# Holding a planner's order on four engines, norms on another engine, and a hidden state laid out by batch, in a four-layer graph network

## The chip, the cores and the metric

The kernel runs on one core of a Trainium2 chip. A core has five engines with a queue each: TensorE (PE; its weight loads are listed as PEld), VectorE (DVE), ScalarE (ACT), GpSimd (POOL) and SyncE (SP), which here issues transfers. The metric is the time of one execution on the device in microseconds (us); the median of three runs before the change is 2407.23 us (2405.26 to 2409.41).

## The reference, cut to what matters

x is 128 batches of 64 nodes with 256 features, adj a 64 by 64 matrix. Four layers follow each other, each as x = layernorm(x + layer(x)):

```python
# layer 0: graph convolution with two batch norms over all 128*64 rows
agg = A_hat @ x;  h = relu(bn(agg @ W1.T + b1));  out = bn(h @ W2.T + b2)
# layer 1: spectral convolution, 4-head attention masked by adj, MLP
h  = relu(ln((L_norm @ x) @ Wc + bc) * g1 + be1);  x1 = h + x
x2 = ln(x1 + attention(x1) @ Wo + bo) * g2 + be2
y  = ln(x2 + gelu(x2 @ W1 + b1) @ W2 + b2) * g3 + be3
# layer 2: two graph convolutions, then four LSTMs one after the other on windows of nodes
h = relu(adj @ (relu(adj @ (x @ Wg0 + bg0)) @ Wg1 + bg1))
for p in 1, 2, 3, 4:       # a window is p neighbouring nodes; its last node gets the LSTM's last state
    h[:, p-1::p] = lstm_p(windows of p nodes of h)
# layer 3: graph attention (one head), residual and norm
```

L_norm needs the largest eigenvalue of a 64 by 64 Laplacian, for which a power of the matrix is formed at the start. All is fp32.

## The kernel before

**Tiles.** The 128 batches are cut into 16 blocks of 8; a block's x is 128 rows by 4 by 256 (`X[i]`, "token-major"), and its hidden state is as large (`H[i]`). Eight spare tiles of the same size (`t`) and, as they come free, tiles of x, h and old weights make up a stock `mem`; PSUM is a stock of four tiles `ps`. The names in the profile are those of the tiles: x, h, t, ps, wA, wB, wL and so on.

**A planner in Python.** The kernel is written as generators ("tasks"): `first_block` and `second_block` (layer 0, a batch norm ends each), `end_block` (layer 0's last norm), `block` (layer 1), `gcn_block` (layer 2's convolutions and LSTM 1 of a block), `unit` (LSTMs 2 to 4 on a group of 32 batches), `last_block` (layer 3). Each `yield step(engine, us, ...)` announces the next piece of work on T (PE), V (VectorE), S (ScalarE), G (POOL) or Q (a transfer) with a cost in us. The loop `flow` keeps up to six blocks in flight, simulates the engines' times by these costs, and always lets that task go on whose next piece can start first; the instructions of the piece are then emitted. It is called twice: for layer 0, and for all the rest. A table change on ScalarE is charged 1.3 us.

**Who sets the order on the chip.** What `flow` emits is a program, not yet the queues. The compiler's scheduler takes the instructions of all engines and orders each engine's queue by its own model of their times; the emitted order is only its priority. In the trace an engine works its queue off in that order, so an instruction that waits for its input holds what stands behind it.

**Norms.** `stats` (L272 to L274) does the statistics on VectorE; then POOL raises the variance to the power -0.5 (L282, L294, L308). Three helpers apply the norm: `ln_steps` (VectorE, L285), `ln_affine_steps` (VectorE, two operations per 256 columns, L297 and L300, with gamma and beta in them), and `ln_steps_act` (a small `ln_nm` on VectorE, L311, then ScalarE, L314). `block` uses `ln_affine_steps` twice, for g1/be1 and g3/be3.

**The hidden state.** From the end of `gcn_block` on, h of a group of 32 batches is one tile seen as `hT`, "p (c n b)": for each of two halves of the features, node by node, with the 32 batches side by side. LSTM 1 writes into it across (L1357, its step is 32 elements). `unit` reads the s-th node of each window (`x_of`) as runs of 32 batches and writes the last node (L1389). PE reads these inputs in the first step's products (L1055), in the product "A11" of the seven products that stand for eight (L1127, a variant of Strassen's method), and in `plain_steps` (L1264). The differences T1 (POOL, L1147) and T3 (VectorE, L1173) read them too. `last_block` copies a block of hT back into batch order with two ScalarE copies (L1467) before it transposes it.

**Lines that the prediction names.** L741: batch norm 2 on ScalarE in `end_block`. L776: relu and residual. L784: copy of the transposed x1. L822, L915, L916, L933: whole-tile operations on POOL. L898: residual after attention. L928: gelu. L1171, L1228: VectorE operations with both inputs in SBUF.

Of the kernel before, what the change touches and what calls it, by code (L numbers as in the profile page):

```python
# [15 lines left out]
P = 128  # L16
# [3 lines left out]
NT = 4  # L20
# [13 lines left out]
def kernel(ctx: ExitStack, tc: tile.TileContext, a: dict, out: bass.AP):  # L34
    nc = tc.nc
    V, S, G, T = nc.vector, nc.scalar, nc.gpsimd, nc.tensor

# [92 lines left out]
    def flow(streams, margin):  # L130
# [92 lines left out]
    hT = [t.rearrange("p (c n b) -> p c n b", c=2, n=N) for t in Hg]  # L223
# [53 lines left out]
    def ln_steps(y):  # L277

        yield step("V", 2.45)
# [3 lines left out]
        yield step("V", 1.9)  # L283
# [5 lines left out]
    def ln_affine_steps(y, g, b):  # L289

        yield step("V", 2.45)
        mv, rs = stats(y)
        yield step("G", 1.0)
        G.tensor_tensor(rs, rs, neghalf[:, :NT], ALU.pow)  # L294
        yield step("V", 3.4)
        for t in range(NT):
            V.scalar_tensor_tensor(y[:, t, :], y[:, t, :], mv[:, t, 0:1], g, ALU.subtract, ALU.mult)  # L297
            o = b if len(b.shape) == 2 else b[:, t, :]
            dst = y if len(b.shape) == 2 else b
            V.scalar_tensor_tensor(dst[:, t, :], y[:, t, :], rs[:, t : t + 1], o, ALU.mult, ALU.add)  # L300

    def ln_steps_act(y):

        n = y.shape[1]
        yield step("V", 0.6 * n)
        mv, rs = stats(y)
        yield step("G", 1.0)
        G.tensor_tensor(rs, rs, neghalf[:, :n], ALU.pow)  # L308
        yield step("V", 0.2)
        nm = sm.tile([P, n], F32, tag="ln_nm", name="ln_nm")  # L310
        V.scalar_tensor_tensor(nm, mv[:, :, 0], -1.0, rs, ALU.mult, ALU.mult)  # L311
        yield step("S", 0.6 * n)
        for t in range(n):
            S.activation(  # L314
                y[:, t, :], y[:, t, :], AF.Identity, scale=rs[:, t : t + 1], bias=nm[:, t : t + 1]
            )
# [89 lines left out]
    with c0:  # L406
# [129 lines left out]
        def bn_coeffs(name, nch, st, g, be):  # L536
# [4 lines left out]
            yield step("V", 0.3 * nch)  # L541
# [16 lines left out]
        def first_block(i):  # L558
# [6 lines left out]
            yield step("T", 1.15, ps=1, sl=1)  # L565
# [25 lines left out]
        def second_block(i):  # L591
# [27 lines left out]
            yield step("S", 2.8)  # L619
# [6 lines left out]
            yield step("V", 1.4, sl=2)  # L626
# [6 lines left out]
            yield step("G", 1.3, waits=False)  # L633
            G.tensor_tensor(T4, h[:, :, u], T2, ALU.subtract)
            yield step("V", 0.7)
# [98 lines left out]
    def end_block(i):  # L734
# [4 lines left out]
        yield step("S", 1.4)  # L739
# [15 lines left out]
    def block(i):  # L755
        x = X[i]
        mark("begun", i)
        yield step("T", 1.15, ps=1, sl=1)
# [15 lines left out]
        yield from ln_affine_steps(y, rows[:, names.index("g1"), :], rows[:, names.index("be1"), :])  # L774
        yield step("V", 1.25)
# [25 lines left out]
        yield step("T", 3.6, ps=1, sl=1)  # L801
# [19 lines left out]
        yield step("G", 2.4, waits=False)  # L821
# [3 lines left out]
        yield step("T", 1.15, ps=1, sl=1)  # L825
# [17 lines left out]
        yield step("V", 1.4, ps=-1)  # L843
# [5 lines left out]
        yield step("V", 2.5)  # L849
# [9 lines left out]
        yield step("G", 1.9)  # L859
# [13 lines left out]
        yield step("T", 1.15, ps=1, sl=1)  # L873
# [40 lines left out]
        yield step("G", 4.7, waits=False)  # L914
# [3 lines left out]
        for hf in range(2):  # L918
# [6 lines left out]
            yield step("S", 1.4, ps=-1, waits=hf == 1, tbl="gelu")  # L925
# [6 lines left out]
        yield step("G", 2.4, waits=False)  # L932
# [17 lines left out]
        yield from ln_affine_steps(y, rows[:, names.index("g3"), :], x)  # L950
# [25 lines left out]
    V.tensor_tensor(bl, bl, bh, ALU.add)  # L976

    def gcn_rows():
# [15 lines left out]
        PS.give(ps)  # L994
        mark("rows")
# [25 lines left out]
    def hT_block(i):  # L1021

        return hT[i // 4][:, :, :, (i % 4) * 8 : (i % 4) * 8 + 8]

    def lstm(p, n, parts, x_of, out_of):
# [4 lines left out]
        v_us, g_us, s_us = (0.05 + n * r for r in (1.25e-3, 2.3e-3, 1.15e-3))  # L1030
# [50 lines left out]
        for c in range(2):  # L1081
            if c:
                tb, sb = yield from gates(((0, 1), (2, 1)), *other)
            t, sl = (tb, sb) if c else (ta, sa)
            t = yield step("G", g_us, at=t, waits=False)
            G.tensor_tensor(of(s_cell)[:, c], of(sl)[:, 0], of(sl)[:, 1], ALU.mult)
            tc_.append(t)
        t_o, s_o = yield from gates(((3, 0), (3, 1)), *to)
        s_h = None
        for c in range(2):  # L1090
# [5 lines left out]
            t = yield step("V", v_us, at=max(t, t_o), sl=0 if p == 1 or c else 1, waits=False)  # L1096
# [39 lines left out]
        for s in range(1, p):  # L1136
# [3 lines left out]
            t_1 = yield step("G", g_us, sl=2, at=0.0, waits=False)  # L1140
# [28 lines left out]
            def differences():  # L1169
                yield step("V", two_us, at=h_at, waits=False)  # L1170
                V.tensor_tensor(T2, h_v, T1, ALU.subtract)  # L1171
                t_h.append((yield step("V", two_us, at=h_at, waits=False)))
                V.tensor_tensor(shaped(T3), shaped(h_v), x_v, ALU.subtract)  # L1173
                t_h.append((yield step("G", g_us, at=t_h[1], waits=False)))
# [44 lines left out]
            t_g = yield step("G", 2 * g_us, at=at[2], waits=False)  # L1219
# [7 lines left out]
            yield step("V", 2 * v_us, at=at[1], waits=False)  # L1227
            V.tensor_tensor(cell, cell, of(act[1]), ALU.mult)  # L1228
            mem.give(act[1])
            t = yield step("V", 2 * v_us, at=t_g, waits=False)  # L1230
# [6 lines left out]
            t = yield step("V", 2 * v_us, at=max(t, at[3]), sl=0 if last else 1, waits=False)  # L1237
# [12 lines left out]
    def plain_steps(p, n, us, of, bias, x_of, shaped, last_h, s_cell, s_h, h_at):  # L1250

        v_us, g_us, s_us = (0.05 + n * r for r in (1.25e-3, 2.3e-3, 1.15e-3))
        for s in range(1, p):
# [20 lines left out]
            for c in range(2):  # L1274
# [4 lines left out]
                tg = yield step("G", g_us, at=ta, waits=False)  # L1279
                G.tensor_tensor(A[:, 1], A[:, 0], A[:, 1], ALU.mult)  # L1280
                t = yield step("V", v_us, at=tb, waits=False)
                V.tensor_tensor(cell, cell, F[:, 0], ALU.mult)
                t = yield step("V", v_us, at=max(t, tg), waits=False)
# [5 lines left out]
            for c, t, sa, sb in ends:  # L1289
                t = yield step("V", v_us, at=t, sl=0 if last or c else 1, waits=False)  # L1290
# [15 lines left out]
    def gcn_block(i):  # L1306
        yield step("T", 1.15, ps=1, sl=1)
# [21 lines left out]
        yield step("T", 1.15, ps=1, sl=1)  # L1329
# [12 lines left out]
        yield step("V", 1.4, ps=-1)  # L1342
# [13 lines left out]
        def out_of(q, c, o, th):  # L1356
            V.tensor_tensor(  # L1357
                hT_block(i)[:, c, :, :].rearrange("p n b -> p b n"), o, th, ALU.mult
            )
# [8 lines left out]
    def unit(p, g, w0, nw, b0, nb):  # L1368
        src = hT[g][:, :, w0 * p : (w0 + nw) * p, b0 : b0 + nb].rearrange("p c (w q) b -> p c w q b", q=p)

        hn = nw * nb // 2
        even = nw % 2 == 0
        parts = [(slice(q * hn, (q + 1) * hn), nw // 2 if even else nw) for q in range(2)]
        if nb < BG:
            parts = [(slice(0, 2 * hn), nw)]

        def half(ap, q):
# [3 lines left out]
            if even:  # L1381
                return ap[..., q * nw // 2 : (q + 1) * nw // 2, :]
            return ap[..., q * nb // 2 : (q + 1) * nb // 2]

        def x_of(s, q):
            return half(src[:, :, :, s, :], q)

        def out_of(q, c, o, th):
            V.tensor_tensor(half(src[:, c, :, p - 1, :], q), o, th, ALU.mult)  # L1389
# [22 lines left out]
    def sum_weights(p, sums):  # L1412
# [18 lines left out]
        for k in range(2):  # L1431
            i0, i1, h0, h1 = (w[:, k, :, c, :] for w in (ih, hh) for c in range(2))
            s1, s2, s3, s4 = (gates(sums[2 * i + k]) for i in range(4))
            for dst, y, z, op in (
# [5 lines left out]
                yield step("V", 0.7)  # L1440
# [15 lines left out]
    def last_block(i, t0=0, nt=NT):  # L1456
# [6 lines left out]
        yield step("S", 2.2 * r, sl=1)  # L1463
        s_h = mem.take()
        hb = fm(mem[s_h])[:, :, : nt * P]
        for c in range(2):
            S.copy(  # L1467
                hb[:, c, :].rearrange("p (b n) -> p b n", n=N),
                hT_block(i)[:, c, :, 2 * t0 : 2 * (t0 + nt)].rearrange("p n b -> p b n"),
            )  # L1470
# [3 lines left out]
        to_tm(px, hb)  # L1474
        mem.give(s_h)
# [13 lines left out]
        yield step("S", 0.3 + 1.1 * r, ps=-1)  # L1489
# [7 lines left out]
        for t in range(0, nt, 2):  # L1497
# [20 lines left out]
            yield step("S", 0.7, ps=-1, waits=False)  # L1518
# [5 lines left out]
        yield step("G", 0.1 + 0.5 * r, sl=1)  # L1524
# [9 lines left out]
        yield step("V", 0.3 + 1.2 * r, ps=-1)  # L1534
# [6 lines left out]
        yield step("S", 0.3 * nt, tbl="exp")  # L1541
# [3 lines left out]
        yield step("V", 0.3 + 0.3 * r)  # L1545
        V.reciprocal(sums[:, :nt], sums[:, :nt])
        V.tensor_tensor(e, e, bc_last(sums[:, :nt], N), ALU.mult)
        yield step("T", 0.1 + 0.5 * r, ps=1)
# [8 lines left out]
        yield step("T", 0.1 + 0.95 * r, ps=1)  # L1557
# [113 lines left out]
    def last_of(i, *part):  # L1671
# [17 lines left out]
        MARGIN,  # L1689
    )  # L1690
# [48 lines left out]
```

## Time and profile before

| what | value |
|---|---|
| median of the runs shown | 2407.23 us (2405.26 to 2409.41) |
| profiled execution: its own time | 2409.44 us |
| profiled execution: span from first to last instruction | 2407.7 us |
| PE busy, of the span | 2287.2 us (95%) |
| VectorE, ScalarE, POOL busy | 1287.7, 1187.4, 591.7 us |
| mean granted clock of PE | 0.982 |
| chain that ended last: PE, VectorE, ScalarE, POOL | 60%, 16%, 7%, 3% |
| ScalarE table loads in the largest group (L928) | 18 of 1283 ns |

Times are read from one profiled execution. A "busy" share is the union of an engine's instructions; a matmul in fp32 stands as two records. The page's slices are fortieths of the span, some 60 us each, with one digit (tenths) per engine; a window gives the same for any stretch. A timeline row is: start, duration, engine, source line, operation, output and inputs, shape, how many are merged, and in brackets how long the engine was idle before and what ended that. "The chain that ended last" is followed back from the last instruction. The clock is what the chip granted PE, as a share of full speed.

### The profile page before, as it was taken

Reading aid. Unit: us, or ns where it says so; the run is one execution under the profiler, and the core shown is the slowest. Engines: PE = TensorE matmul, PEld = TensorE weight load, DVE = VectorE, ACT = ScalarE, POOL = GpSimd, SP = SyncE. Lnnn points to the kernel's source line nnn. Section 1 sums busy time; section 2 is a strip of 40 time slices with the busy share of each in tenths; the row PEclk is TensorE's granted clock in tenths of the full one; section 3 lists DMA queues with packets and bytes.
Section 4 is the critical chain, followed back from the end, with each engine's and each line's share of the span. In section 5 each row is a group of like instructions: output and inputs, shape, how many; then the busy total and the mean of one; then the engine's idle time right before and its main releaser. Section 6 shows DMA issues by size and latency. Waiting matters only on the chain.

```text
span 2407.7 us, 40603 instructions
## 1 busy us (share of the span) xinstructions
PE 2287.2 (95%) x16916; PEld 1759.9 (73%) x16916; DVE 1287.7 (53%) x2904; ACT 1187.4 (49%) x2189; POOL 591.7 (25%) x441
## 2 busy tenths in 40 slices
PE   8999788999989999999999999999999999998997
PEld 4548665666665666666667788899999888887785
DVE  4557678566483474744643433454444444455546
ACT  2257643544434544335453443444444653468766
POOL 0012134232242232331321222222221222122122
PEclk9999899999999999999999999999999999999998
DMA  6100301000000000001000000000001000001111
GB/s 162 49 1 1 111 23 49 28 10 10 1 12 17 10 10 10 1 10 36 36 19 27 18 1 1 17 2 1 1 1 36 1 10 9 19 27 66 40 36 45
DMA packets 42633, 57.91 MB, mean 24 GB/s; under 512 B 6224, under 2 KB 35536, under 8 KB 42448
## 3 DMA queue, kind: packets, MB, share of 16 engines
q1 hardware_dynamic: 41344, 54.22, 7.0%
q8 instruction: 133, 2.18, 0.4%
q10 hardware_dynamic: 1104, 1.08, 0.1%
q14 instruction: 52, 0.43, 0.1%
HBM read 38.52 MB, written 16.78 MB: 23 GB/s over the span
## 4 chain that ended last, share of the span: by engine, by line
PE 60%; DVE 16%; ACT 7%; POOL 3%; issue 2%; POOLq 0%; ACTq 0%; DVEq 0%
PE ps L1127 26%; PE ps L1055 11%; PE ps L365 7%; PE ps L377 4%; PE ps L938 4%; DVE ln_st L272 3%; ACT x L314 2%; PE ps L808 2%; POOL ln_rs L308 1%; PE ps L1507 1%; DVE x L300 1%; PE ps L341 1%; DVE ln_mv L273 1%; PE ps L353 1%; DVE ln_nm L311 1%
## 5 line engine op out<-in xcount | busy, mean ns | idle before, releaser
L1127 PE MATMUL ps<-x,x 128*128 128x256 f32 x928 | 225.0, 380 | 0.7 <-DVE t L1195 0.7
L1127 PEld LDWEIGHTS ps<-x,x 128*128 128x128 f32 x928 | 173.5, 190 | 24.9 <-issue 1.6
L314 ACT ACTIVATE x<-x,ln_nm,ln_rs 128x256 f32<-128x256 f32 x212 | 112.3, 592 | 133.3 <-DVE ln_nm L311 131.9
L1127 PE MATMUL ps<-t,x 128*128 128x256 f32 x672 | 163.7, 380 | 0.0
L1127 PEld LDWEIGHTS ps<-t,x 128*128 128x128 f32 x672 | 126.4, 190 | 17.1 <-DVE x L1195 0.8
L308 POOL TENSOR_TENSOR ln_rs<-ln_rs,neghalf 128x4 f32<-128x4 f32 (+1 forms) x72 | 71.2, 990 | 212.0 <-DVE ln_rs L274 186.4
L365 PE MATMUL ps<-t,W1T 128*128 128x512 f32 x256 | 117.8, 607 | 0.0
L1055 PE MATMUL ps<-h,wL 128*128 128x192 f32 (+2 forms) x480 | 103.9, 371 | 4.8 <-ACT h L1353 4.8
L272 DVE BATCH_NORM_STATS2 ln_st<-x 128x6 f32<-128x256 f32 x260 | 99.7, 403 | 0.4
L1055 PEld LDWEIGHTS ps<-h,wL 128*128 128x128 f32 x480 | 75.6, 192 | 29.9 <-issue 22.5
L294 POOL TENSOR_TENSOR ln_rs<-ln_rs,neghalf 128x4 f32<-128x4 f32 x32 | 36.9, 1153 | 217.1 <-DVE ln_rs L274 217.0
L1055 PE MATMUL ps<-h,x 128*128 128x256 f32 x384 | 86.7, 380 | 2.2 <-ACT t L1067 1.8
L1067 ACT ACTIVATE t<-ps,bih 128x512 f32<-128x512 f32 (+3 forms) x98 | 57.2, 634 | 55.8 <-PE ps L1055 55.1
L1203 ACT ACTIVATE x<-x,bih 128x512 f32<-128x512 f32 (+2 forms) x69 | 44.6, 648 | 80.3 <-DVE x L1193 80.0
L1186 DVE COPY x<-ps 128x256 f32<-128x256 f32 (+2 forms) x69 | 26.1, 378 | 108.4 <-PE ps L1127 107.6
L365 PEld LDWEIGHTS ps<-t,W1T 128*128 128x128 f32 x256 | 47.6, 195 | 49.6 <-issue 49.5
L365 PE MATMUL ps<-t,wA 128*128 128x512 f32 x160 | 76.8, 626 | 5.5 <-ACT t L784 5.5
L1055 PEld LDWEIGHTS ps<-h,x 128*128 128x128 f32 x384 | 72.6, 190 | 12.9 <-ACT t L1067 2.2
L1186 DVE COPY t<-ps 128x256 f32<-128x256 f32 (+2 forms) x51 | 18.8, 373 | 103.8 <-PE ps L1127 103.5
L1067 ACT ACTIVATE x<-ps,bih 128x512 f32<-128x512 f32 (+3 forms) x86 | 51.5, 650 | 40.6 <-PE ps L1055 40.4
L273 DVE BATCH_NORM_AGGREGATE ln_mv<-ln_st 128x2 f32<-128x6 f32 x448 | 71.3, 167 | 0.0
L1193 DVE TENSOR_TENSOR x<-ps,x 128x512 f32<-128x512 f32 (+2 forms) x69 | 41.4, 602 | 53.0 <-PE ps L1127 43.6
(714 smaller groups left out, 5713.2 us busy)
## 6 DMA issues: line engine op xcount, KB each, us to landing
t<-in_x_dram SPq DMA_DIRECT2D x26, 512.0 KB, 4.3
xd<-x SPq DMA_DIRECT2D x16, 512.0 KB, 2.6
x<-xd SPq DMA_DIRECT2D x8, 512.0 KB, 3.3
out_dram<-x SPq DMA_DIRECT2D x8, 512.0 KB, 2.9
h<-in_x_dram SPq DMA_DIRECT2D x5, 512.0 KB, 5.2
wL<-in_L_gnn_Wih_dram SPq DMA_DIRECT2D x2, 1024.0 KB, 5.0
x<-in_L_gnn_Whh_dram SPq DMA_DIRECT2D x2, 1024.0 KB, 5.4
x<-xd SPq DMA_DIRECT2D x5, 256.0 KB, 2.9
```

The costliest lines, as they stand in the source:

```text
L272: V.bn_stats(st[:, t, :], y[:, t, :])
L273: V.bn_aggr(mv[:, t, :], st[:, t, :])
L308: G.tensor_tensor(rs, rs, neghalf[:, :n], ALU.pow)
L314: S.activation(y[:, t, :], y[:, t, :], AF.Identity, scale=rs[:, t : t + 1], bias=nm[:, t : t + 1])
L365: T.matmul(ps[:, c, :], w[:, k, (off + c) * P : (off + c + 1) * P], yT[:, k, :], start=(k == 0), stop=(k == nk - 1),)
L377: T.matmul(ps[:, t, :], yT[:, k, t * P : (t + 1) * P], w[:, k, :], start=(k == 0), stop=(k == nk - 1),)
L808: T.matmul(pv[r * N : (r + 1) * N, b, :, :], x1T[:, k, b * N : (b + 1) * N], Wv_par[:, k, r, :, :], start=(k == 0), stop=(k == 1),)
L938: T.matmul(tm(PS[ps])[:, t, :], fm(mem[gs[k // 2]])[:, k % 2, t * P : (t + 1) * P], W2[:, k, :], start=(k == 0), stop=(k == 3),)
L1055: T.matmul(spread(fm(PS[ps])[:, j, :n], q), WL[p][0][:, k, m], x_of(0, q)[:, k], start=(k == 0), stop=(k == 1),)
L1067: S.activation(of(sl)[:, j], fm(PS[ps])[:, j, :n], AF.Tanh if g == 2 else AF.Sigmoid, bias=bias(g, c))
L1127: T.matmul(dst, WS[p][name](k, g), y[:, k], start=first and k == 0, stop=k == 1, skip_group_check=not first)
L1186: V.tensor_copy(y[:, 1, :], v[:, 0, :])
```

## The change

Five things, of which only the first three change what is executed; the others change the planner's choices.

1. **The order of emission is held** on PE, VectorE, ScalarE and POOL: the compiler's scheduler no longer reorders these queues. SP's queue is still the scheduler's.
2. **Layer 1's norms go to ScalarE**: `ln_affine_steps` is gone; `ln_steps_act` is used, and gamma and beta follow as whole-tile operations on VectorE.
3. **h by batch**: `hT` becomes "p (c b n)": for each batch its 64 nodes side by side. LSTM 1 writes it contiguously; `unit` reads and writes every p-th element; units are halved by batches; `last_block` needs no copy, its two ScalarE copies and their tile are gone.
4. **The planner knows two more things.** Steps of VectorE and POOL that are tagged "m" (two SBUF inputs) don't start on VectorE while a tagged POOL step runs. A change of the matmuls' shape ("quarter", "columns" or whole) is charged 0.1 us. The second `flow` starts its clocks where layer 0 ended instead of at 0.
5. **Costs are adjusted** in some thirty steps, by up to a few tenths of a us each. The sum of two LSTM biases is emitted later, in `gcn_rows`.

The diff, cut to its core:

```diff
+    E = mybir.EngineType
+    ctx.enter_context(tc.manual_schedule(engines={E.PE, E.DVE, E.Activation, E.Pool}))
...
-        free = dict.fromkeys("TVSGQ", 0.0)
-        table, running, now, seq = None, [], 0.0, 0
+        free = dict.fromkeys("TVSG", start) | {"Q": 0.0}
+        table, shape, locked, running, now, seq = None, None, start, [], 0.0, 0
...
+                if e == "V" and tbl == "m":
+                    t, soon = max(t, locked), max(soon, locked)
...
-            if tbl is not None and tbl != table:
+            if e == "S" and tbl is not None and tbl != table:
                 us, table = us + 1.3, tbl
+            if e == "T" and tbl != shape:
+                us, shape = us + 0.1, tbl
+            if e == "G" and tbl == "m":
+                locked = when + us
...
-    hT = [t.rearrange("p (c n b) -> p c n b", c=2, n=N) for t in Hg]
+    hT = [t.rearrange("p (c b n) -> p c b n", c=2, n=N) for t in Hg]
...
     def ln_steps_act(y):
         n = y.shape[1]
-        yield step("V", 0.6 * n)
+        yield step("V", 0.3 + 0.53 * n)
         mv, rs = stats(y)
         yield step("G", 1.0)
         G.tensor_tensor(rs, rs, neghalf[:, :n], ALU.pow)
         yield step("V", 0.2)
         nm = sm.tile([P, n], F32, tag="ln_nm", name="ln_nm")
         V.scalar_tensor_tensor(nm, mv[:, :, 0], -1.0, rs, ALU.mult, ALU.mult)
-        yield step("S", 0.6 * n)
+        yield step("S", 0.1 + 0.5 * n)
...
# block(i), first norm
-        yield from ln_affine_steps(y, rows[:, names.index("g1"), :], rows[:, names.index("be1"), :])
-        yield step("V", 1.25)
+        yield from ln_steps_act(y)
+        yield step("V", 3.7, tbl="m")
+        V.tensor_tensor(y, y, row["g1"], ALU.mult)
+        V.tensor_tensor(y, y, row["be1"], ALU.add)
         V.scalar_tensor_tensor(y, y, 0.0, x, ALU.max, ALU.add)
...
# block(i), last norm
-        yield from ln_affine_steps(y, rows[:, names.index("g3"), :], x)
+        yield from ln_steps_act(y)
+        yield step("V", 2.45, tbl="m")
+        V.tensor_tensor(y, y, row["g3"], ALU.mult)
+        V.tensor_tensor(x, y, x, ALU.add)
...
# gcn_block(i), LSTM 1
-            V.tensor_tensor(
-                hT_block(i)[:, c, :, :].rearrange("p n b -> p b n"), o, th, ALU.mult
-            )
+            V.tensor_tensor(hT_block(i)[:, c], o, th, ALU.mult)
...
     def unit(p, g, w0, nw, b0, nb):
-        src = hT[g][:, :, w0 * p : (w0 + nw) * p, b0 : b0 + nb].rearrange("p c (w q) b -> p c w q b", q=p)
+        src = hT[g][:, :, b0 : b0 + nb, w0 * p : (w0 + nw) * p].rearrange("p c b (w q) -> p c b w q", q=p)
...
         def x_of(s, q):
-            return half(src[:, :, :, s, :], q)
+            return half(src[..., s], q)
...
# last_block(i, t0, nt)
-        yield step("S", 2.2 * r, sl=1)
-        s_h = mem.take()
-        hb = fm(mem[s_h])[:, :, : nt * P]
-        for c in range(2):
-            S.copy(
-                hb[:, c, :].rearrange("p (b n) -> p b n", n=N),
-                hT_block(i)[:, c, :, 2 * t0 : 2 * (t0 + nt)].rearrange("p n b -> p b n"),
-            )
         yield step("T", 0.9 * r, ps=1)
         ps = PS.take()
         px = tm(PS[ps])[:, :nt, :]
-        to_tm(px, hb)
-        mem.give(s_h)
+        to_tm(px, hT_block(i)[:, :, 2 * t0 : 2 * (t0 + nt)].rearrange("p c b n -> p c (b n)"))
```

More of the change, by code (lines that the diff above doesn't have):

```diff
@@ L277, in ln_steps @@
     def ln_steps(y):
-        yield step("V", 2.45)
+        yield step("V", 2.43)
         mv, rs = stats(y)
@@ L798, in block @@
         qT, kT = fm(mem[qk[0]]), fm(mem[qk[1]])
-        yield step("T", 3.6, ps=1, sl=1)
+        yield step("T", 3.6, ps=1, sl=1, tbl="columns")
         ps = PS.take()
@@ L913, in block @@
         PS.give(ps)
-        yield step("G", 4.7, waits=False)
+        yield step("G", 4.7, waits=False, tbl="m")
         G.tensor_tensor(y, y, row["g2"], ALU.mult)
@@ L924, in block @@
                 mem.give(s_x2)
-            yield step("S", 1.4, ps=-1, waits=hf == 1, tbl="gelu")
+            yield step("S", 1.27, ps=-1, waits=hf == 1, tbl="gelu")
             for c in range(2):
@@ L931, in block @@
             PS.give(ps)
-        yield step("G", 2.4, waits=False)
+        yield step("G", 2.4, waits=False, tbl="m")
         G.tensor_tensor(x, x, row["be3"], ALU.add)
@@ L994, in gcn_rows @@
         PS.give(ps)
+        V.tensor_tensor(bl, bl, bh, ALU.add)
         mark("rows")
@@ L1236, in lstm @@
             S.activation(of(act[2]), cell, AF.Tanh)
-            t = yield step("V", 2 * v_us, at=max(t, at[3]), sl=0 if last else 1, waits=False)
+            t = yield step("V", 2 * v_us, at=max(t, at[3]), sl=0 if last else 1, waits=False, tbl="m")
             if last:
@@ L1289, in plain_steps @@
             for c, t, sa, sb in ends:
-                t = yield step("V", v_us, at=t, sl=0 if last or c else 1, waits=False)
+                t = yield step("V", v_us, at=t, sl=0 if last or c else 1, waits=False, tbl="m")
                 if last:
@@ L1689 @@
         MARGIN,
+        start=done["bn2",],
     )
```

109 lines of the change are left out of this document (47 added, 62 removed).

## The prediction

> **What bounds the kernel now.** I read the page's busy shares first, then its forty slices, then the windows by stage, then the waits of TensorE (PE) and the timeline around the longest of them.
>
> ```profile
> PE 2287.2 (95%) x16916; PEld 1759.9 (73%) x16916; DVE 1287.7 (53%) x2904; ACT 1187.4 (49%) x2189; POOL 591.7 (25%) x441
> PE   8999788999989999999999999999999999998997
> PEclk9999899999999999999999999999999999999998
> ```
>
> PE is busy for 95% of the span. No matmul goes away in this change, so all it can win is PE's idle time, 2408.0 - 2287.2 = 120.8 us, and the time that PE worked below full clock. The windows (span of the stage; busy us of PE, PEld, VectorE = DVE, ScalarE = ACT, POOL; granted clock; DMA) say where that lies:
>
> ```profile
> 240.00:300.00 60.00, 45.18 (x320) 37.66 (x319) 36.20 (x96) 39.18 (x66) 8.70 (x12) 0.87 0.35 111
> 300.00:360.00 60.00, 52.61 (x658) 38.08 (x660) 43.65 (x108) 27.75 (x40) 21.21 (x14) 0.90 0.08 23
> 360.00:420.00 60.00, 49.38 (x314) 34.25 (x304) 50.62 (x113) 23.37 (x37) 26.56 (x16) 0.94 0.15 49
> 960.00:1080.00 120.00, 110.64 (x1049) 75.54 (x1039) 76.11 (x140) 47.08 (x58) 43.23 (x24) 0.97 0.03 10
> 1320.00:1440.00 120.00, 120.00 (x533) 100.45 (x532) 49.22 (x81) 50.03 (x98) 28.57 (x18) 1.00 0.03 10
> 2160.00:2220.00 60.00, 51.16 (x357) 42.17 (x356) 34.97 (x112) 53.93 (x121) 10.81 (x12) 0.97 0.22 72
> 2340.00:2408.00 68.00, 49.94 (x338) 38.18 (x336) 36.89 (x160) 43.86 (x110) 14.02 (x22) 0.90 0.12 40
> ```
>
> PE's idle time by stage is the window less its busy time: 18.7 us in 0-240 (layer 0), 32.8 in 240-420 (layer 1 starts), 0 in 420-480, 32.3 in 480-1320 (layers 1 and 2 together), 4.4 in 1320-2160 (LSTM, PE full), 32.6 in 2160-2408 (tail); sum 120.8. Work at a lower clock costs busy x (1 - clock): 5.9 + 5.3 + 3.0 = 14.2 in 240-420, 11.4 in 480-1320, 6.5 in 2160-2408, 6.2 in layer 0. The low clocks stand in the stages with idle time, so they shrink with it.
>
> In 240-420 the waits of PE name VectorE and ScalarE, not data from memory: four gaps of 4.3, 5.5, 5.5 and 4.7 us, ended by L776, L784, L898 and L928. This is the second:
>
> ```profile
> 318.03 2.34 POOL L822 TENSOR_TENSOR t<-t,rows 128x1024 f32<-128x1024 f32 x1
> 318.09 2.29 DVE L311 SCALAR_TENSOR_TENSOR ln_nm<-ln_mv,ln_rs 128x4 f32<-128x4 f32 x1 [0.86 <-POOL ln_rs L308]
> 320.42 2.07 ACT L314 ACTIVATE x<-x,ln_nm,ln_rs 128x256 f32<-128x256 f32 x4 [4.59 <-DVE ln_nm L311]
> 322.40 0.99 ACT L784 COPY t<-ps 128x1024 f32<-128x1024 f32 x1
> 323.44 1.22 PE L365 MATMUL ps<-t,wA 128*128 128x512 f32 x1 [5.53 <-ACT t L784]
> ```
>
> A four-column operation on VectorE, 0.16 us elsewhere, lasts as long as the POOL operation that began just before it; the norm on ScalarE waits for it; the copy L784, whose input PE had ready at 317.9, stands behind the norm; PE stands behind the copy. Two more signs of the same:
>
> ```profile
> 286.55 11.40 ACT L741 ACTIVATE h<-h,bn2sh,bn2sc 128x512 f32<-128x512 f32 x16
> ...
> 710.01 2.34 POOL L822 TENSOR_TENSOR x<-x,rows 128x1024 f32<-128x1024 f32 x1
> 710.07 5.85 DVE L300 SCALAR_TENSOR_TENSOR x<-x,ln_rs,x 128x256 f32<-128x256 f32 x4 [0.51 <-POOL ln_rs L294]
> 712.32 2.53 POOL L916 TENSOR_TENSOR h<-h,rows 128x1024 f32<-128x1024 f32 x1
> ```
>
> The sixteen L741 belong to eight different blocks, and the planner has at most six in flight; here ScalarE does them in one run of 11.4 us. So the order on the chip isn't the planner's: the compiler's own ordering pulled them forward. And four L300, about 0.48 us each undisturbed, take 5.85 us beside two POOL operations.
>
> **The change part by part.**
>
> **Norms of layer 1.** Off VectorE go 128 L297 (70.7 us) and 128 L300 (81.0 us, by windows of those lines) = 151.7. On it come 32 small ln_nm (L311, mean 0.376: 12.0 us) and 64 whole-tile operations (two rows per norm), priced by L1228, which also has two SBUF inputs of 1024: 1.22 x 64 = 78.1. VectorE saves 61.6 us, 10.6 of them in 240-420 (there the two lines have 26.0; x (1 - 90.1/151.7)). ScalarE gets 128 x 0.592 (L314) = 75.8 us. A norm's own chain gets longer: before 8 x 0.48 = 3.8 us, after 0.2 + 2.4 + 2.45 = 5.0, plus a hand-over. What hides that is the six blocks in flight; without them it would be 32 x 1.3 = 42 us. As price on PE I take 0 and count the gain below, with the order.
>
> **h by batch.** ScalarE loses L1467: 33.9 us, of which 12.4 in 2160-2220, 4.6 and 4.5 in the two last stages. VectorE's 32 writes L1357 become contiguous: 1.06 to 0.69 (L1171, same shape) = -11.8 us. In exchange, units of step p read their inputs with p elements from one to the next, 8, 12 or 16 bytes, where they had runs of 32 elements. On VectorE and POOL that hits 33 L1147, 33 L1173 and the 80 writes L1389. The rows that show a far step:
>
> ```profile
> L1357 DVE TENSOR_TENSOR h<-x,t x8: 1035/1063/2515, 567.0 to 1356.7; 128x512 f32<-128x512 f32 x8
> L1467 ACT COPY x<-h x12: 636/1089/1117, 1859.6 to 2373.6; 128x512 f32<-128x512 f32 x10, 128x256 f32<-128x256 f32 x2
> L1353 ACT ACTIVATE t<-t x6: 1056/1057/1057, 545.9 to 1321.1; 128x1024 f32<-128x1024 f32 x6
> ```
>
> The columns are minimum/median/maximum in ns. A step of 128 bytes doubles ScalarE's time per element (1.09 us for 512 against 1.06 for 1024) and makes VectorE's 1.54 times as long. At a doubling POOL gets +40 us and VectorE +60 in a stage where they are busy 24% and 41%: hidden, 0; at 0 us nothing happens either.
>
> On PE it is not hidden. The records that read h this way have 256 columns in p=4 (528: 48 of a unit's first step and 3 x 16 of product A11, three units; 240 of the two plain units) and 192 or 144 in p=3 (320 each). At the pitch of the chain's stretch "PE ps L1127 x168", 36.26 us, that is 0.216 us for 256 columns: p=4 is 114 us, p=3 51.8 + 39.2 = 91, p=2 (512 records) 110. No row shows PE reading with a step, so bounds: below 0 there is nothing, since the columns stay; above, PE at ScalarE's 2.1 ns per far element instead of 0.84 would add 1.5 x (114 + 91) = 308 us. I take 0, because the nearest rows by engine, PE's L1264 with runs of 16 elements and L1127 with runs of 32, have the pitch of contiguous ones; the other end is rival 2.
>
> [...]
>
> **Order held, with the new model.** PE gains where VectorE and ScalarE brought a ready result late. By the timeline, L784 could have come 4 us earlier, L898 (input ready at 367.4, run at 375.95) all of its 5.5, L928 about 4; L776 found VectorE full. Not all is won: another step is late in its place, and the model does not tag the ln_nm step or the stats, though the row at 318.09 shows ln_nm held 2.3 us; and there will be 104 of these, not 72. So I take half of the 20.1 us, with a little for the lighter VectorE: -11 in 240-420, and half of 480-1320: -16. Clock in proportion (11/32.8 of 14.2; 16/32.3 of 11.4): -5 and -6. Bounds: 0 (the gaps move), and -65 with the clock's -25 if all of both go. 1320-2160: -1 of 4.4. Layer 0: 0; its gaps (7.0 us for the first load, 5.8 at the first batch norm) are data that nobody has earlier.
>
> **Tail.** In 2160-2220 ScalarE is busy 53.9 of 60 and its copies L1467 are 12.4; PE's 8.8 us of idle time are ended by ScalarE for the most part: -6. Behind 2220 the copies of the last chunks are on the path, two of 0.57 (half of the halved tile) twice: -3. All 32.6 can't go: the last chain of norm, scores, softmax and norm stays.
>
> **Sum.** -11 - 16 - 5 - 6 - 1 - 6 - 3 = -48 us against the profiled execution's 2409.4: 2361; the median of the runs shown is 2.2 lower (2407.23), so 2359.
>
> **Rivals.**
> 1. *The gaps only move*: the order is held, but unforeseen holds (ln_nm, stats) now stop all that stands behind on the same queue, which the compiler's order would have gone around; the longer norm chain does the rest. For: VectorE 84% busy in 360-420, ScalarE gets 76 us. Against: PE was already fed for 420-480 and 1320-1800 without a gap. Only the tail's -9 and a few us of new gaps: about 2404, between 2400 and 2412.
> 2. *PE pays for the step in h* (the slower side): if PE's time per column doubles with a far step, as ScalarE's per element does in L1467, and only the widest step, that of p=4, counts as far, +114: 2359 + 114 = 2473; if p=3 pays half as much more (+46), 2519. For: L1467 and L1357. Against: no row shows that PE's pace of 0.84 ns per column is set by its reads. It decides from 48/114: a pitch of 0.216 x 1.42 = 0.307 us for 256 columns.
> 3. *The order doesn't bite*: if PE's order and timing hardly differ, parts two and tail alone give 2395.
>
> **How the numbers follow.** Forecast 0.66 (2359, its own range 2325 to 2392), rival 3 0.05 (2395), rival 1 0.07 (2400 to 2412, five in seven of it within 0.2%, about what a measurement of this kernel can tell from no change), rival 2 0.22 (2415 to 2530, 2473 likeliest). Range 2325 to 2475: it leaves out some 4 in 100 below and 10 above. Faster by over 0.2% (under 2402.4): 0.66 + 0.05 + 0.01 = 0.72; same: 0.05; slower: 0.22 + 0.01 = 0.23.
>
> **What would show it.** Right: PE's idle time in 240-420 near 20 us, in 480-1320 near 16; L741 in pairs; no L1467; ScalarE near 1230 us and VectorE near 1215. Wrong: 1320-2160 still full but longer, with L1127 reading h at a longer pitch in p=4 or p=3 (rival 2); a PE gap ended by ScalarE or VectorE whose queue stood behind one held instruction (rival 1).

## The result, and the profile after

The changed kernel takes 2594.95 us (median of 4, 2593.97 to 2597.14), the kernel before 2407.24 us beside it: a ratio of 1.0781 [1.0762, 1.0799], so 188 us slower. The forecast was 2359, its range ended at 2475.

The page of the changed kernel (busy us of the span's 2593.8):

```profile
PE 2464.7 (95%) x16916; PEld 1804.9 (70%) x16916; DVE 1287.8 (50%) x2744; ACT 1215.5 (47%) x2277; POOL 614.7 (24%) x441
```

PE executes the same 16916 records and is busy 177.5 us longer. Its idle time is 129.1 us against 120.5. So the lost time is not waiting: the matmuls themselves last longer. The windows of the changed kernel (columns as in the prediction) say what became of the idle time:

```profile
240.00:300.00 60.00, 42.80 (x305) 35.40 (x303) 39.10 (x95) 26.30 (x47) 9.66 (x12) 0.85 0.34 111
300.00:360.00 60.00, 54.77 (x683) 41.24 (x684) 50.01 (x118) 37.39 (x56) 16.54 (x12) 0.92 0.14 41
360.00:420.00 60.00, 55.29 (x384) 36.10 (x382) 48.31 (x102) 40.69 (x63) 26.36 (x16) 1.00 0.13 43
480.00:960.00 480.00, 479.48 (x4560) 320.59 (x4559) 283.88 (x544) 255.31 (x350) 156.48 (x94) 1.00 0.03 10
1080.00:1200.00 120.00, 109.58 (x876) 78.54 (x874) 60.91 (x120) 53.70 (x78) 32.10 (x21) 0.96 0.07 25
1320.00:1440.00 120.00, 118.83 (x517) 96.90 (x516) 47.99 (x80) 45.78 (x92) 27.64 (x17) 1.00 0.03 9
```

PE's idle time is 27.1 us in 240-420 (32.8 before) and 17.2 in 480-1320 (32.3 before, 17.2 = 0.5 + 3.1 + 10.4 + 3.2 in four windows). Most of the gain that was hoped for there exists: 20.8 of 27 us, although 1080-1200 alone got worse, from 2.2 to 10.4. But 1320-1440, which had no gap, has one of 1.2 us, and 1320-2160 as a whole 21.9 instead of 4.4.

How the matmuls got longer is seen in a plain step of p = 4, where h is the moving input. The records overlap: four of them last 1.03 us in the first row below, and the next four start 0.86 us after the start of these. What counts is the time from one start to the next. The kernel before, then the changed one:

```profile
2237.23 1.03 PE L1264 MATMUL ps<-h,wB 128*128 128x256 f32 x4
2238.09 1.03 PE L1266 MATMUL ps<-t,x 128*128 128x256 f32 x4
```

```profile
2381.07 2.00 PE L1265 MATMUL ps<-h,wB 128*128 128x256 f32 x4
2382.89 1.82 PE L1267 MATMUL ps<-h,x 128*128 128x256 f32 x4
```

Four records lie between the two starts each time: 0.86 us before, 0.215 each; 1.82 us after, 0.455 each. Over all records from start to start, medians: 256 columns some 450 ns in p = 4 (216 before), 192 columns 259 (163), 144 columns 213 (123) in p = 3, 216 to 224 in p = 2 (216). With the counts of the prediction: 528 x 0.234 + 320 x 0.096 + 320 x 0.090 = 124 + 31 + 29 = 184 us, near the 177.5 by which PE's busy time grew.

### The profile page after: what moved, and what is told of

Read it like the earlier page. It is cut to its first block, busy times and chain, and to the rows that moved or that the text cites. A ratio compares the mean times of both kernels' runs of the same rounds, so it can differ in the third digit from the quotient of the medians.

```text
span 2593.8 us, 40514 instructions
## 1 busy us (share of the span) xinstructions
PE 2464.7 (95%) x16916; PEld 1804.9 (70%) x16916; DVE 1287.8 (50%) x2744; ACT 1215.5 (47%) x2277; POOL 614.7 (24%) x441
## 5 line engine op out<-in xcount | busy, mean ns | idle before, releaser
L304 POOL TENSOR_TENSOR ln_rs<-ln_rs,neghalf 128x4 f32<-128x4 f32 (+1 forms) x104 | 107.8, 1037 | 532.1 <-DVE ln_rs L283 485.8
L1128 PE MATMUL ps<-t,x 128*128 128x256 f32 x800 | 201.8, 386 | 1.4 <-DVE x L1196 1.1
L1128 PE MATMUL ps<-x,x 128*128 128x256 f32 x768 | 187.3, 382 | 1.5 <-DVE t L1196 0.6
L1128 PEld LDWEIGHTS ps<-t,x 128*128 128x128 f32 x800 | 152.7, 194 | 33.9 <-issue 10.5
L1128 PEld LDWEIGHTS ps<-x,x 128*128 128x128 f32 x768 | 145.3, 192 | 29.3 <-issue 8.0
L1056 PE MATMUL ps<-h,wL 128*128 128x192 f32 (+2 forms) x480 | 135.8, 445 | 1.8 <-ACT t L1208 1.3
L1056 PEld LDWEIGHTS ps<-h,wL 128*128 128x128 f32 x480 | 94.0, 197 | 36.9 <-issue 20.8
L1068 ACT ACTIVATE t<-ps,bih 128x512 f32<-128x512 f32 (+2 forms) x96 | 57.0, 644 | 111.4 <-PE ps L1056 109.1
L1265 PE MATMUL ps<-h,wB 128*128 128x256 f32 x192 | 95.1, 629 | 0.0
L1056 PE MATMUL ps<-h,wB 128*128 128x256 f32 x192 | 88.0, 629 | 0.0
L1194 DVE TENSOR_TENSOR t<-ps,t 128x512 f32<-128x512 f32 (+2 forms) x64 | 38.4, 599 | 89.6 <-PE ps L1128 75.6
L1128 PE MATMUL ps<-h,wL 128*128 128x144 f32 (+1 forms) x256 | 72.3, 411 | 9.0 <-ACT x L1208 3.4
L1128 PE MATMUL ps<-h,wB 128*128 128x256 f32 x144 | 72.1, 635 | 8.9 <-ACT t L1506 1.9
```

Source lines behind the costliest of these rows:

```text
L1056: T.matmul(spread(fm(PS[ps])[:, j, :n], q), WL[p][0][:, k, m], x_of(0, q)[:, k], start=(k == 0), stop=(k == 1),)
L1068: S.activation(of(sl)[:, j], fm(PS[ps])[:, j, :n], AF.Tanh if g == 2 else AF.Sigmoid, bias=bias(g, c))
L1128: T.matmul(dst, WS[p][name](k, g), y[:, k], start=first and k == 0, stop=k == 1, skip_group_check=not first)
L1194: V.tensor_tensor(y[:, 0:2, :], v[:, 2:4, :], y[:, 0:2, :], ALU.add)
L1265: T.matmul(shaped(dst), WL[p][0][:, k, m], x[:, k], start=(k == 0), stop=False)
```

## The experiments

**1. The layout undone.** The changed kernel with h by node again and the two ScalarE copies back; the rest of the change stays.

```diff
-    hT = [t.rearrange("p (c b n) -> p c b n", c=2, n=N) for t in Hg]
+    hT = [t.rearrange("p (c n b) -> p c n b", c=2, n=N) for t in Hg]
...
+        for c in range(2):
+            S.copy(hb[:, c, :]..., hT_block(i)[:, c, :, 2 * t0 : 2 * (t0 + nt)].rearrange("p n b -> p b n"))
```

> The changed kernel with h by node again (runs of 32 batches) and the two ScalarE copies back; held order, new model and norms stay. Theory S (PE pays for the step in h, 183 us by the records of the changed kernel's trace: 528 of 256 columns at 450 instead of 216 ns, 320 at 259 instead of 163, 320 at 213 instead of 123): all of that goes, and PE's idle time behind 1080 us, which grew because the planner doesn't know the slow records, goes too: 2355 to 2385 us. Theory O (the held order makes new waits, the step costs little): 2450 or more. In between, near 2410: the step costs 183 us and the order wins nothing.

Measured: 2430.28 us, ratio 1.009 [1.0073, 1.0107]. 165 of the 188 us are the layout's. But the other parts together don't win: they cost 23 us. The time lies in none of the three ranges expected.

**2. The layout alone.** The kernel before with h by batch and without the copies, nothing else.

> The kernel before with h by batch alone (no copies, units halved by batches); order, model and norms as before. Theory S: 2407 + 183 - some 9 in the tail = 2560 to 2600 us. Theory O: 2390 to 2450.

Measured: 2575.67, ratio 1.0698 [1.0682, 1.0714], +168 us, inside theory S's range. PE is busy 2465.2 us, as in the changed kernel. The two runs enclose the price from both sides, 165 and 168.

**3. The step by itself.** A small kernel that leaves the whole computation out and only repeats matmuls and copies whose input has 1, 2, 3, 4, 8 or 32 elements from one read to the next.

```python
for s in (1, 2, 3, 4, 8, 32):          # moving input with a step; then the same as weights
    for k in range(32):
        T.matmul(ps, wts[:, k % 2, :P], every(s, D), start=k == 0, stop=k == 31)
```

> Leaves the whole computation out; its output is the input. It measures the step by itself: on PE 32 products of 128x256 per step with a moving operand of step 1, 2, 3, 4, 8 and 32 elements, then weights read with these steps; on ScalarE, VectorE (reading, then writing) and POOL operations of 512 elements with the same steps. Theory S with 16-byte lines: PE's pitch per record 216 ns at 1 and 2, about 340 at 3, 450 at 4, and no more at 8 and 32. Rival (the cost grows with the distance, as in banks): 8 and 32 clearly above 4. Rival (PE is slow only for the pattern of three nested loops in the kernel, not for a plain step): 216 throughout. Weights: open, 190 ns at 1; up to 1.76 ns per column, 225 ns, if lines limit them too.

The timeline of PE; the outputs movea to movef are the steps 1, 2, 3, 4, 8, 32, and load is the part with stepped weights:

```profile
40.08 13.98 PE L62 MATMUL movea<-src,wts 128*128 128x256 f32 x64
53.89 14.67 PE L62 MATMUL moveb<-src,wts 128*128 128x256 f32 x64
68.40 21.92 PE L62 MATMUL movec<-src,wts 128*128 128x256 f32 x64
90.15 29.04 PE L62 MATMUL moved<-src,wts 128*128 128x256 f32 x64
119.01 29.62 PE L62 MATMUL movee<-src,wts 128*128 128x256 f32 x64
148.45 27.91 PE L62 MATMUL movef<-src,wts 128*128 128x256 f32 x64
176.19 43.11 PE L66 MATMUL load<-wts,src 128*128 128x256 f32 x192
```

From one start to the next, by 64 records: 216, 227, 340, 451, 460 and 433 ns. Theory S holds and both rivals fell: a plain step is enough (340 ns at three elements, 451 at four), and steps of 8 and 32 elements (460 and 433 ns) cost what a step of four (16 bytes) does. An estimate that fits these six pitches to within 4%: the larger of 0.84 ns per column (216 / 256) and 1.76 ns per stretch of 16 bytes that is read (451 / 256, at step 4). 256 columns touch 128, 192 and 256 such stretches at steps of 2, 3 and 4, which gives 225, 338 and 451, where 227, 340 and 451 were measured. For the kernel's 192 and 144 columns at step 3 it gives 253 and 190, where 259 and 213 were measured; why the second is 12% over isn't shown. The last row is the other half of the finding: 192 records with the same steps in the weights take 43 us, 0.22 each (216 to 238). The weight loads themselves get longer (187 to 337 ns), but beside 256 moving columns the steps in the stationary input cost at most 22 of 216 ns per record. ScalarE's copy of 512 went 0.62, 0.68, 0.90, 1.14, 1.14, 1.22 us over the six steps, VectorE's operation 0.69, 0.69, 0.86, 1.10, 1.11, 1.16, POOL's 1.28, 1.32, 1.43, 1.53, 1.52, 1.53.

**4. The step in the stationary input.** h by node as in experiment 1, but the last layer's transposes read it as weights with a step of 32 elements; no copies. The planner's cost of the step is adapted (2.0 instead of 0.9).

```diff
-        to_tm(px, hb)
+        for t in range(nt):
+            for c in range(2):
+                for q in range(2):
+                    T.matmul(px[halves[q], t, c * P : (c + 1) * P], hb[:, c, :, 2 * (t0 + t) + q], ident, ...)
```

> As e1_old_layout, but without the copies: the last layer's transposes load h by node as weights, 64 columns with a step of 32 elements, in two halves of PE. If weight loads with a step hide beside the matmuls: 5 to 15 us below e1_old_layout, by what the copies cost the tail. If PE pays for them (2 halves x 2 x 128 loads x up to 0.1 us): up to 20 us above it.

Measured: 2410.34, ratio 1.001 [1.0001, 1.002], 20 us better than experiment 1 and more than the 5 to 15 expected, although PE is busy 7.9 us longer (2297.1 against 2289.2). So the copies were worth 20 us here, and they can go without the layout; without the hold the same pair differs by 12 (experiments 7 and 6 below). The layout's balance comes out: 184 lost on PE, some 20 won, 165 measured.

**5 to 8. The hold, the costs and where the hold ends.** Still open: why the rest costs 23 us.

5: the kernel before with `manual_schedule` on the four engines, that line alone. 6: experiment 1 without that line. 7: experiment 4 without it. 8: experiment 4 with the hold (`hold`, opened by hand at the start) left when the last block ends layer 1. On the chip that is near 1310 us: up to there PE's records stand in the same order in 4 and 8.

```diff
         mark("l1", i)
+        if all(("l1", j) in done for j in range(NBLK)):
+            hold.__exit__(None, None, None)
```

> The kernel before with one line of the change alone: the order of emission held on the four engines; old costs, old norms, old layout, both copies. Theory A (the hold itself costs what the old layout's run lost, 23 us: it wins some 25 us before 1080 us and loses some 50 behind): 2415 to 2440, with PE idle 50 us or more behind 1320 and gaps ended by L1207. Theory B (the new costs and the norms on ScalarE lose the 23, the hold wins): at or under 2400. If the old costs make a poor order to hold, it is worse than 2440.

> The run with the old layout and the two copies (2430), without the hold: new costs and norms on ScalarE, the compiler orders the queues. Theory A (the hold is what wins before 1080 us and loses behind): 2400 to 2412, PE's idle time behind 1320 back near 37 us, in 240 to 1080 near 58. Theory B (the costs and norms lose): stays at 2425 or more.

> The run with h by node whose last layer takes it as weights with a step, without copies (2410), without the hold. Theory A: 2385 to 2398, what the run without the hold gives less some 10 to 20 us for the copies. Theory B: 2405 or more.

> The run with h by node read as weights (2410), with the hold only until the last block leaves layer 1; the compiler orders what follows. Theory A (gain before 1080 us and loss behind are two separate things): 2360 to 2385, PE's idle time in 480 to 1080 under 10 us and behind 1320 under 50. Theory C (the early gain is a debt: what was won is idle time later, whoever orders): 2395 to 2412. Theory B: 2405 or more.

Measured:

| experiment | us | ratio to before |
|---|---|---|
| 5, hold alone | 2428.69 | 1.0087 [1.0072, 1.0102] |
| 6, experiment 1 without the hold | 2465.03 | 1.0239 [1.0222, 1.0256] |
| 7, experiment 4 without the hold | 2453.41 | 1.019 [1.0175, 1.0206] |
| 8, hold to the end of layer 1 | 2379.64 | 0.9883 [0.9868, 0.9898] |

The fifth agrees with theory A. The sixth and seventh lie in theory B's open ranges, but far above the 23 us that both theories set out to explain: without the hold the new planner and norms cost some 58. So the hold alone costs 21, the rest alone 58, both together 23: they don't add. The eighth is inside theory A: the hold wins in front and loses behind the end of layer 1, and the two can be separated. Windows of experiment 4 (held to the end), then of experiment 8:

```profile
1320.00:1560.00 240.00, 237.39 (x1093) 202.83 (x1092) 94.01 (x159) 97.24 (x205) 52.61 (x34) 1.00 0.03 9
1800.00:2040.00 240.00, 227.05 (x1321) 199.31 (x1321) 105.23 (x233) 111.14 (x257) 53.85 (x41) 1.00 0.04 14
```

```profile
1320.00:1560.00 240.00, 240.00 (x1141) 208.90 (x1140) 107.44 (x178) 103.08 (x209) 54.55 (x37) 1.00 0.03 9
1800.00:2040.00 240.00, 235.51 (x1375) 206.16 (x1374) 114.96 (x254) 117.54 (x274) 60.62 (x44) 0.99 0.04 14
```

In 480-960 the two are alike (PE idle 0.8 and 0.5 us, 16.4 in the kernel before). Behind 1320 the held kernel has gaps of 2.6 and 13.0 us in these two stretches, the other 0 and 4.5, and it gets through more matmuls in each. Over the span PE is idle 112.1 and 85.0 us.

**9. The norms alone.** The kernel before with layer 1's two norms on ScalarE, old costs, the compiler's order.

> The kernel before with layer 1's two norms on ScalarE and gamma and beta as whole-tile operations on VectorE, and nothing else: old costs, compiler's order, h by node. Without the hold, costs and norms together cost 57 us. Theory N (the longer norm chain, with the copies of the same engine behind it, costs most of it): 2435 to 2465, PE's gaps in 480 to 1080 ended by ScalarE. Theory M (the new costs give the compiler an order that it handles worse, the norms are harmless): 2400 to 2415.

Measured: 2424.45, ratio 1.0066 [1.0049, 1.0083], +16 us: between the two theories. VectorE is busy 1224.0 us, 63.7 less than before.

**10, 11, 13, 14. Which queue loses behind layer 1.** All as experiment 8, but behind layer 1 the hold goes on for some engines: without ScalarE (10), without VectorE (11), without both (13), without PE (14).

```diff
             hold.__exit__(None, None, None)
+            ctx.enter_context(tc.manual_schedule(engines={E.DVE, E.Activation, E.Pool}))   # 14: PE free
```

> Held to the end on PE, VectorE and POOL, but on ScalarE only to the end of layer 1 (2410 with all four held to the end, 2380 with none behind layer 1). Theory S (the loss behind layer 1 stands on ScalarE's held queue: the activation that frees PSUM behind the tanh and the next product's copy): 2380 to 2388, the 1.25 us gaps gone. Theory D (it stands on VectorE's queue: h behind the statistics of a norm): 2402 to 2410.

> The same with VectorE free behind layer 1 and ScalarE held. Theory S: 2402 to 2410, the 1.25 us gaps remain. Theory D: 2380 to 2388, the 4.4 us gaps behind statistics gone, the others left. If both queues have a share, both runs lie between.

> Behind layer 1 only PE and POOL stay held, VectorE and ScalarE are free (all four held 2410; ScalarE free 2406; VectorE free 2399; all free 2380). Theory V (the two queues lose together, each covering for the other): 2380 to 2386. Theory P (PE's held order loses the rest): 2393 to 2400.

> Behind layer 1 only PE is free; VectorE, ScalarE and POOL stay held. Theory V: 2403 to 2412. Theory P: 2385 to 2395.

| held behind layer 1 | us | ratio to before |
|---|---|---|
| PE, VectorE, ScalarE, POOL (4) | 2410.34 | 1.001 [1.0001, 1.002] |
| PE, VectorE, POOL (10) | 2406.23 | 0.9986 [0.9977, 0.9996] |
| PE, ScalarE, POOL (11) | 2399.31 | 0.9962 [0.9947, 0.9976] |
| PE, POOL (13) | 2398.08 | 0.9959 [0.9944, 0.9974] |
| VectorE, ScalarE, POOL (14) | 2384.44 | 0.9901 [0.9886, 0.9915] |
| none (8) | 2379.64 | 0.9883 [0.9868, 0.9898] |

Freeing PE alone wins 26 of the 31 us; freeing VectorE and ScalarE wins 12, so the two don't add. Theories S and D both fell (run 10 lies where D has it, run 11 where neither does), theory V too; P holds, with run 14 a little better than it said. The view of waits would have misled here. The largest wait of PE in 1320-2300 of experiment 4 (total us, times, longest) names ScalarE:

```profile
PE ps L1128 <- ACT t L1208: 5.8, 8, 1.3
```

and the timeline shows such a wait: L1208 is the last reader of a PSUM tile, and it stands behind L1168 and L1206.

```profile
1756.44 0.36 ACT L1168 COPY t<-ps 128x256 f32<-128x256 f32 x1
1756.69 0.46 ACT L1206 ACTIVATE x<-x,bih 128x192 f32<-128x192 f32 x1
1757.05 0.42 ACT L1208 ACTIVATE x<-ps,bih 128x192 f32<-128x192 f32 x1
1757.52 0.92 PE L1128 MATMUL ps<-h,wL 128*128 128x192 f32 x4 [1.25 <-ACT x L1208]
```

Yet with ScalarE free PE's waits for this line go on (11.1 us in all tiles in run 10, 17.6 in experiment 4), and with PE free they nearly end (1.3 us in run 14). PE's idle time behind 1320 is 49.0 us in experiment 4, 44.2 in 10, 41.1 in 13, 28.5 in 14 and 23.8 in 8. What the compiler does with PE's queue is seen in the traces. In 4, 10, 11 and 13 PE's 17300 records stand in the same order throughout; in 14 some 270 of them stand elsewhere, the first near 1310 us. One such place, in run 10 and then in run 14 (L1132 and L1212 are L1128 and L1208 of experiment 4):

```profile
1752.99 0.81 PE L1132 MATMUL ps<-x,wA 128*128 128x192 f32 x4
1754.64 0.92 PE L1132 MATMUL ps<-h,wL 128*128 128x192 f32 x4 [0.84 <-ACT x L1212]
```

```profile
1743.81 1.53 PE L1132 MATMUL ps<-x,x 128*128 128x256 f32 x6
1745.18 0.87 PE L1132 MATMUL ps<-h,wL 128*128 128x192 f32 x4
```

In run 10 the products of h and wL come directly behind those of x and wA and wait 0.84 us for ScalarE. In run 14 six records of a later product stand between the two, and no wait is left. Elsewhere the waits that vanish so were ended by VectorE (0.81 us behind L1107 near 1654 us of run 10). So a local move of a few records fills a gap, whichever engine ends it; that this is all of the 26 us isn't shown.

**12. The statistics of a norm grouped.** Experiment 8 with all `bn_stats` of a norm ahead of its `bn_aggr`.

```diff
         for t in range(n):
             V.bn_stats(st[:, t, :], y[:, t, :])
+        for t in range(n):
             V.bn_aggr(mv[:, t, :], st[:, t, :])
```

> The run held to the end of layer 1 (2380), with all bn_stats of a norm emitted ahead of its bn_aggr instead of one after the other. Held, they alternate at 0.53 us per 256 columns; the compiler's own order in the kernel before had 0.39. If that carries over, each of some 130 held norms ends 0.5 us sooner: VectorE less by 30 to 60 us, its statistics' idle time less, PE's idle time in 240 to 420 and 960 to 1200 a few us less: 2368 to 2378. If PE does not wait there: 2378 to 2382.

Measured: 2368.08, ratio 0.9833 [0.9818, 0.9848], inside the range of the first reading, 12 us better than experiment 8 and the fastest of all. The held order is the emitted one, also where it is a poor one. VectorE's timeline of one norm in experiment 8, then in 12:

```profile
369.71 0.41 DVE L282 BATCH_NORM_STATS2 ln_st<-t 128x6 f32<-128x256 f32 x1
370.15 0.18 DVE L283 BATCH_NORM_AGGREGATE ln_mv<-ln_st 128x2 f32<-128x6 f32 x1
370.25 0.39 DVE L282 BATCH_NORM_STATS2 ln_st<-t 128x6 f32<-128x256 f32 x1
...
371.95 0.17 DVE L284 TENSOR_SCALAR ln_rs<-ln_mv 128x4 f32<-128x4 f32 x1
```

```profile
364.54 1.39 DVE L282 BATCH_NORM_STATS2 ln_st<-t 128x6 f32<-128x256 f32 x4
365.86 0.35 DVE L284 BATCH_NORM_AGGREGATE ln_mv<-ln_st 128x2 f32<-128x6 f32 x4
366.24 0.69 DVE L285 TENSOR_SCALAR ln_rs<-ln_mv 128x4 f32<-128x4 f32 x1
```

From the first to the operation behind the last: 2.24 us against 1.70. VectorE's busy time falls from 1282.6 to 1243.2 us, PE's idle time in 360-420 from 3.6 to 0.5.

**15 and 16. Costs and norms apart.** 15: the kernel before with the new planner alone: the costs, the two rules, the later start of the second `flow`'s clocks, and the sum of the LSTM biases emitted later. 16: the same with the hold. Both have the old norms and layout.

> The new costs and the planner's two new rules alone: old norms on VectorE, h by node with the copies, the compiler's order. The norms alone cost 17 us, costs and norms together 57. If the two add up: 2440 to 2455. If the loss needs both (a longer norm chain that the new planner mistimes): 2407 to 2425.

> Costs, rules and hold with the old norms on VectorE, h by node with the copies (2430 with the new norms). If the norms on ScalarE cost 17 under the hold too: 2408 to 2418. If they gain under the hold, as the lighter VectorE should (50 us less): 2435 to 2450, VectorE near 90 percent busy in 300 to 420. If they are worth nothing: 2427 to 2433.

Measured: 2465.24 (1.0238 [1.0223, 1.0253]) and 2437.04 (1.0127 [1.011, 1.0144]). Neither expectation of 15 foresaw that the new planner alone brings all of the 58 us. 16 lies in its second range: the norms on ScalarE are worth 7 us under the hold. VectorE is busy 85% in 300-420 there, where near 90 was expected. The table (us, all with h by node and the copies; "costs" stands for all that 15 changes):

| | compiler's order | order held to the end |
|---|---|---|
| old costs, old norms | 2407 | 2429 (5) |
| old costs, norms on ScalarE | 2424 (9) | not run |
| new costs, old norms | 2465 (15) | 2437 (16) |
| new costs, norms on ScalarE | 2465 (6) | 2430 (1) |

**17. The old order held to the end of layer 1.** Experiment 5 with the hold left there.

> The kernel before with the hold alone, and that only to the end of layer 1: old costs, old norms, old layout, copies (2429 with the hold to the end). If the hold's loss behind layer 1 is independent of the costs, some 30 us come back: 2393 to 2402, faster than before by what PE's idle time in 240 to 1080 lost (12 us). If only the new costs' order is worth holding: 2405 to 2425.

Measured: 2394.79, ratio 0.9939 [0.9923, 0.9956], as the first reading has it. The hold's loss behind layer 1 is 34 us with the old costs, 31 with the new ones: it hardly depends on the costs. In front PE's idle time in 240-1080 falls from the kernel before's 58.6 us by 12 with the old costs (to 46.7) and by 27 with the new costs and norms (to 31.7, in experiment 1).

## Why the prediction was wrong, step by step

**"h by batch ... I take 0, because the nearest rows ... have the pitch of contiguous ones."** This step failed, and it carries 184 of the 236 us between forecast and measurement; the other 52 are the gain of 48 that did not come and 4 more. L1264 and L1127 had runs of 16 and 32 elements, which is four reads of every 16 bytes; they could say nothing on one read per 16 bytes. Experiment 3 has 216 ns for 256 columns at four reads per 16 bytes, 227 at two, 340 at 1.33 and 451 at one. The rows on far steps (L1357, L1467) were from other engines (1.54 and 2.06 times the time per element); PE's 451 ns is 2.09 times its 216. Shown by experiments 1, 2 and 3: PE's pitch (from one record's start to the next) rose from 216 to some 450 ns at p = 4, over the 307 from which rival 2 was to decide. The bounds, 0 to 308, held it.

**Rival 2**, at 0.22, named what the runs show: PE pays for the step in h. Its +114 for p = 4 measured 124. For p = 3 it had 0 or 46, measured 60: no run shows its assumption that only the widest step counts as far (192 columns took 259 ns at p = 3, 163 before). It stood at 2473 or 2519 since it kept the forecast's gain of 48, which did not come either. (Rival 3's 2395 doesn't follow from the sum: the tail's -9 alone gives 2398.)

**Order, 240-420 and 480-1320.** Right in kind, half the size in 240-420: "near 20" and "near 16" us of PE's idle time were 27.1 and 17.2; won are 5.7 and 15.1 where -11 and -16 stood. The clock's share, busy x (1 - clock), fell from 14.2 to 10.8 and from 11.4 to about 7, where -5 and -6 stood. L741 (L737 after) stands in runs of four, two blocks each, instead of one of sixteen; "in pairs" was expected.

**Order, behind 1320: "-1 of 4.4".** The second failed step, of the kind of rival 1, but with another place and price: the hold costs 31 to 34 us there (experiments 8 and 17). With the new costs 26 of the 31 come back when PE's queue alone is free (14); with the old ones this wasn't run. The argument "PE was already fed for 1320-1800 without a gap" was read as safety. By run 14 it was the compiler's reordering of PE's queue that kept it fed. The prediction looked for harm in VectorE's and ScalarE's queues, and for benefit in all four; it never asked what the hold takes from PE.

**New costs and rules.** The sum had no term for what they do to the order. Under the compiler's order they cost 58 us (15): PE's idle time grows by 41 us, 27 of them in 480-1320 and 12 behind 1320, and its busy time by 15, at a mean clock of 0.968 against 0.982. Under the hold they cost 8 with the old norms (experiments 5 and 16). Which of the some thirty costs does it, or one of the rules, the later start or the moved sum, stays open.

**Norms, "as price on PE I take 0".** +16 alone with the old costs, 0 with the new ones unheld, -7 held: no single price, but small. VectorE's -61.6 measured -63.7 in experiment 9. In the changed kernel VectorE stands at 1288 instead of 1215: held, it is busy 54 us longer (1231.7 unheld in experiment 6, 1285.4 held in 1). By the traces 34 of them are the statistics, which alternate in the held order (299 us against 265); the other 20 weren't followed up. ScalarE's 1230 measured 1216.

**Tail, -9.** Too small, and not only in the tail: without the copies 20 us are won under the hold (experiment 4 against 1), although the transposes gain 384 records. PE's idle time falls by 14 us behind 2160 and by 14 in 1320-2160, where the sum counted nothing for the copies.

## What to carry to other kernels

Before a layout is turned, count for each matmul how many reads of its moving input fall on the same 16 bytes: here 256 columns in fp32 took 227 ns at two, 340 at 1.33 and 451 at one (experiment 3). Where the price was high, it helped to move the step to the stationary input (216 to 238 ns per record), or to an engine that has time left (VectorE's write L1357, 1.06 us instead of 0.69). A planner's order can be held for a stretch: hold it where the profile shows results brought late, and let the compiler order the stretch that is full; ask of each held queue what its reordering did so far, that of the bottleneck engine above all. The engine that a wait names is not always the queue to change.

## What the runs showed of the hardware

All of this is experiment 3, in fp32. PE's records of 256 moving columns followed each other at 216, 227, 340, 451, 460 and 433 ns at steps 1, 2, 3, 4, 8 and 32: 0.84 ns per column at step 1, 0.89 at step 2, 1.33 at step 3, 1.76 at step 4 and 1.69 to 1.80 beyond. With the same steps in the weights a record took 216 to 238 ns beside 256 moving columns. A step of 32 took ScalarE's copy of 512 from 0.62 to 1.22 us, VectorE's operation from 0.69 to 1.16 and POOL's from 1.28 to 1.53.
